# Quantized feed-forward: each engine's instructions in a written order, five turns deep, and square roots taken from the square sums

## The chip, the core and the metric

The kernel runs as one program on one core of a Trainium2 chip. A core has several engines with instruction queues of their own: TensorE (PE in the profile; PEld are its weight loads), VectorE (DVE), ScalarE (ACT), GpSimd (POOL), and SyncE (SP), which here issues DMA transfers. Each engine takes its instructions in the order of its own queue, and engines wait for each other on semaphores. The metric is the time of one execution on the device in microseconds; lower is better. Beside the times there is one profiled execution, from which every row below comes.

## The reference

The whole computes a two-layer network on `x` (64 x 64 tokens of 256 features): a conditioned scan with attention, a feed-forward, an RNN with a state-space block, and two mixtures of experts. The change is in the first feed-forward, whose input is the residual modulated by a condition and whose two linear layers work on values and weights quantized on the fly:

```python
def _L0_cond2_ref(Efou, y, weight):
    ys = y * (1.0 / np.sqrt(np.float32(weight.shape[0])))
    d = jax.lax.rsqrt(jnp.einsum('bi,io->bo', ys * ys, weight * weight) + 1e-08)
    return jnp.einsum('bsi,io->bso', Efou * ys[:, None, :], weight) * d[:, None, :]

def _L0_ffn_ref(x, norm1_w, w1, act_scale, act_bias, norm2_w, w2):
    def rmsnorm(x, w):
        v = jnp.mean(jnp.square(x), axis=-1, keepdims=True)
        return x * jax.lax.rsqrt(v + 1e-08) * w
    def activation_quant(x):
        scale = 127.0 / jnp.clip(jnp.max(jnp.abs(x), axis=-1, keepdims=True), 1e-5, None)
        return jnp.clip(jnp.round(x * scale), -128, 127) / scale
    def weight_quant(w):
        scale = 1.0 / jnp.clip(jnp.mean(jnp.abs(w)), 1e-5, None)
        return jnp.clip(jnp.round(w * scale), -1, 1) / scale
    def bitlinear(x, norm_w, w):
        return jnp.einsum('bsd,hd->bsh', activation_quant(rmsnorm(x, norm_w)), weight_quant(w))
    h = bitlinear(x, norm1_w, w1)
    h = act_scale * jnp.square(jax.nn.relu(h)) + act_bias
    return bitlinear(h, norm2_w, w2)
...
x = x + _L0_ffn_ref(_L0_cond2_ref(x, cond_1024, L0_cond2_weight), ...)
```

The hidden layer has 1024 features. There are 4096 tokens.

## The kernel before

The residual lives in SBUF as `xT`, features on the partitions, all 4096 tokens beside each other. The stage `ffn0` works on 16 *pairs*: a pair is two tiles of 128 tokens (`T = 2`, four of the 64 batch entries). For each pair seven steps run:

- `product` (lines 614 to 636): GpSimd multiplies the pair's part of `xT` by the condition into `xs` (L617); TensorE multiplies `xs` by the fp32 weight `Wc` (L628) and, beside it in the same PSUM bank, spreads the rows of `d` over the tokens with a 64-wide product against the identity (L632); ScalarE copies that `d` part to `dt` (L634), VectorE multiplies the two into `gm` (L635), and ScalarE makes the square sums of `gm` (`square_sums`, L581).
- `quantize_in`: `quantized` (L584 to L612) on `gm`, 256 wide.
- `turn`: four bf16 transposes on TensorE (L645) and a copy by ScalarE to `qT` (L647).
- `up`: for each of the two tiles two 512-wide bf16 products with `w1q` (L655), each evicted by ScalarE with a Relu scaled by `back1` (L656); then ScalarE's square (L658) and VectorE's activation scale and bias (L659); after both tiles the square sums of `h` (L581).
- `quantize`: `quantized` on `h`, 1024 wide.
- `turn_back`: for each tile eight transposes (L670) and ScalarE's copy to `q2T` (L671).
- `down`: for each tile eight products with `w2q` (L678), ScalarE's scaled eviction `o` (L680), two fp32 transposes (L682); then VectorE adds the result to `xT` (L684) and SyncE sends the pair to `x_mid` in HBM (L685).

`quantized` holds small columns of per-token numbers in one tile `st`: GpSimd makes `v`, the mean square (L592); ScalarE its root (L593); VectorE the reciprocal (L594); five GpSimd instructions refine that by one Newton step and make the largest allowed scale `most` (L595 to L599). VectorE multiplies by the norm weight (L600), takes the largest magnitude (L601), makes the scale from it and `most` (L603, L604); GpSimd makes the factor `back` of the later eviction (L605, L606); VectorE scales and rounds (two L609) and writes the bf16 result (L611).

The steps are written as a pipeline seven turns deep: in a turn, `down` of one pair comes first and `product` of the pair six later comes last. That is the order in which the program asks for the work. The framework's scheduler then sets the order in each engine's queue from its own estimate of when things are ready, so the queues interleave several pairs differently from the text. PSUM has two rings of four banks, `ps` (`product`, `turn`, `up`) and `acc` (`turn_back`, `down`). Tiles of `f2` have two buffers, those of `f3` (`st`, `h`) three.

The stage before is attention, whose memory the stage takes over; behind it comes the RNN, which needs the whole residual (its first products, L723, read all of `xT`).

Of the kernel before, what the change touches and what calls it, by code (L numbers as in the profile page):

```python
# [13 lines left out]
F32 = mybir.dt.float32  # L14
BF16 = mybir.dt.bfloat16
I32 = mybir.dt.int32
AF = mybir.ActivationFunctionType
ALU = mybir.AluOpType
AX = mybir.AxisListType
PSUM = bass.MemoryType.PSUM  # L20

P = 128
B, L, D = 64, 64, 256
# [53 lines left out]
def bank(g, shape=(P, CH), dt=F32, tag="ps"):  # L77
    tag = g.tag or tag
    return g.psum.tile(list(shape), dt, tag=tag, name=tag)
# [452 lines left out]
def ffn0_prepared(g, pool, w):  # L532

    nc = g.nc
    ones = pool.tile([P, P], F32, name="ones")
    nc.gpsimd.memset(ones, 1.0)
    w.w1q, w.m1, one = ternary(g, pool, w.w1, ones, "w1")
    w.w2q, w.m2, two = ternary(g, pool, w.w2, ones, "w2")

    w.ys = ys = pool.tile([P, KD, B], F32, name="ys")  # L540
    ysq = pool.tile([P, KD, B], F32, name="ysq")
    wsq = pool.tile([P, KD, D], F32, name="wsq")
    w.d = d = pool.tile([B, D], F32, name="d")
    d2 = pool.tile([B, 2, D], F32, name="d2")

    def squares():
        nc.vector.tensor_scalar(ys, g.condT, 1.0 / math.sqrt(D), None, ALU.mult)
        nc.vector.tensor_mul(ysq, ys, ys)
        nc.vector.tensor_mul(wsq, w.Wc, w.Wc)

    def sums():
        ps = bank(g)
        for k in range(KD):
            nc.tensor.matmul(ps[:B, :D], ysq[:, k, :], wsq[:, k, :], start=(k == 0), stop=(k == KD - 1))
        nc.vector.tensor_scalar(d2[:, 0, :], ps[:B, :D], EPS, None, ALU.add)

    return chain(one, two, (squares, sums)), (lambda: rsqrt(nc, d2[:, 0, :], d, d2[:, 1, :]),)


def ffn0(g, w):  # L560


    nc, tc = g.nc, g.tc
    F = w.F
    NF = F // P
    T = 2
    TP = T * P
    NP = NT // TP
    BP = TP // L
    with (  # L570
        tc.tile_pool(name="f1", bufs=1) as p1,
        tc.tile_pool(name="f2", bufs=2) as p2,
        tc.tile_pool(name="f3", bufs=3) as p3,
    ):
        w1q, m1, w2q, m2, ys, d = w.w1q, w.m1, w.w2q, w.m2, w.ys, w.d

        def square_sums(x, n):
            ss = p2.tile([P, T], F32, name=f"ss{n}")
            for t in range(T):
                junk = p1.tile([P, n], BF16, name=f"junk{n}")  # L580
                nc.scalar.activation(junk, x[:, t, :], AF.Square, accum_out=ss[:, t : t + 1])  # L581
            return ss

        def quantized(x, ss, wn, mean, n):  # L584

            st = p3.tile([P, 7, T], F32, name=f"st{n}")  # L590
            v, rs, t, most, am, sc, back = (st[:, i, :] for i in range(7))
            nc.gpsimd.tensor_scalar(v, ss, 1.0 / n, EPS, ALU.mult, ALU.add)  # L592
            nc.scalar.activation(rs, v, AF.Sqrt)  # L593
            nc.vector.reciprocal(rs, rs)  # L594
            nc.gpsimd.tensor_mul(t, rs, rs)  # L595
            nc.gpsimd.tensor_mul(t, t, v)
            nc.gpsimd.tensor_scalar(t, t, -0.5, 1.5, ALU.mult, ALU.add)
            nc.gpsimd.tensor_mul(rs, rs, t)
            nc.gpsimd.tensor_scalar(most, rs, 127.0 / 1e-5, None, ALU.mult)  # L599
            nc.vector.tensor_tensor(x, x, wn.unsqueeze(1).to_broadcast([P, T, n]), ALU.mult)  # L600
            nc.vector.tensor_reduce(am, x, AX.X, ALU.max, apply_absolute_value=True)  # L601

            nc.vector.reciprocal(sc, am)  # L603
            nc.vector.scalar_tensor_tensor(sc, sc, 127.0, most, ALU.mult, ALU.min)  # L604
            nc.gpsimd.tensor_mul(back, am, rs)  # L605
            nc.gpsimd.tensor_scalar(back, back, 1e-5, mean, ALU.max, ALU.mult)  # L606
            q = p2.tile([P, T, n], BF16, name=f"q{n}")
            for i in range(T):
                nc.vector.tensor_scalar(x[:, i, :], x[:, i, :], sc[:, i : i + 1], MAGIC, ALU.mult, ALU.add)  # L609

            nc.vector.tensor_scalar(q, x, MAGIC, 127.0, ALU.subtract, ALU.min)  # L611
            return q, back  # L612

        def product(p, v):
            tok = ts(p, TP)
            xs = p2.tile([P, KD, BP, L], F32, name="xs")
            nc.gpsimd.tensor_tensor(  # L617
                xs,
                g.xT[:, :, tok].rearrange("p k (b l) -> p k b l", l=L),
                ys[:, :, ts(p, BP)].unsqueeze(3).to_broadcast([P, KD, BP, L]),  # L620
                ALU.mult,
            )
            xs2 = xs.rearrange("p k b l -> p k (b l)")
            gm = p2.tile([P, T, D], F32, name="gm")
            for t in range(T):
                ps = bank(g, (P, 2, D))
                for k in range(KD):
                    nc.tensor.matmul(ps[:, 0, :], xs2[:, k, ts(t, P)], w.Wc[:, k, :], start=(k == 0), stop=(k == KD - 1))  # L628

                for j in range(2):  # L630
                    b = p * BP + 2 * t + j
                    nc.tensor.matmul(ps[ts(j, L), 1, :], g.ident[:B, b : b + 1].to_broadcast([B, L]), d, start=True, stop=True)  # L632
                dt = p2.tile([P, D], F32, name="dt")
                nc.scalar.copy(dt, ps[:, 1, :])  # L634
                nc.vector.tensor_mul(gm[:, t, :], ps[:, 0, :], dt)  # L635
            v.gm, v.ss1 = gm, square_sums(gm, D)

        def quantize_in(p, v):
            v.q1, v.back1 = quantized(v.gm, v.ss1, w.n1, m1, D)

        def turn(p, v):
            pt = bank(g, (P, KD, TP), BF16)
            for t in range(T):
                for k in range(KD):
                    nc.tensor.transpose(pt[:, k, ts(t, P)], v.q1[:, t, ts(k, P)], g.identb)  # L645
            v.qT = p2.tile([P, KD, TP], BF16, name="qT")
            nc.scalar.copy(v.qT, pt)  # L647

        def up(p, v):
            v.h = p3.tile([P, T, F], F32, name="h")  # L650
            for t in range(T):
                for f in range(F // CH):
                    ps = bank(g)
                    for k in range(KD):
                        nc.tensor.matmul(ps, v.qT[:, k, ts(t, P)], w1q[:, k, ts(f, CH)], start=(k == 0), stop=(k == KD - 1))  # L655
                    nc.scalar.activation(v.h[:, t, ts(f, CH)], ps, AF.Relu, scale=v.back1[:, t : t + 1])  # L656
                h = v.h[:, t, :]
                nc.scalar.activation(h, h, AF.Square)  # L658
                nc.vector.tensor_scalar(h, h, w.act[:, 0:1], w.act[:, 1:2], ALU.mult, ALU.add)  # L659
            v.ss = square_sums(v.h, F)  # L660

        def quantize(p, v):
            v.q2, v.back2 = quantized(v.h, v.ss, w.n2, m2, F)

        def turn_back(p, v):
            v.q2T = p2.tile([P, T, NF, P], BF16, name="q2T")
            for t in range(T):
                pt = bank(g, (P, NF, P), BF16, tag="acc")
                for f in range(NF):
                    nc.tensor.transpose(pt[:, f, :], v.q2[:, t, ts(f, P)], g.identb)  # L670
                nc.scalar.copy(v.q2T[:, t], pt)  # L671

        def down(p, v):
            po = bank(g, (P, KD, TP), tag="acc")
            for t in range(T):
                ps = bank(g, tag="acc")
                for f in range(NF):
                    nc.tensor.matmul(ps[:, :D], v.q2T[:, t, f, :], w2q[:, f, :], start=(f == 0), stop=(f == NF - 1))  # L678
                o = p2.tile([P, D], F32, name="o")
                nc.scalar.activation(o, ps[:, :D], AF.Copy, scale=v.back2[:, t : t + 1])  # L680
                for k in range(KD):
                    nc.tensor.transpose(po[:, k, ts(t, P)], o[:, ts(k, P)], g.ident)  # L682
            x = g.xT[:, :, ts(p, TP)]
            nc.vector.tensor_add(x, x, po)  # L684
            nc.sync.dma_start(g.x[:, :, ts(p, TP)], x)  # L685

        stages = (product, quantize_in, turn, up, quantize, turn_back, down)
        pairs = [SimpleNamespace() for _ in range(NP)]
        for turn_ in range(NP + len(stages) - 1):
            for i in reversed(range(len(stages))):  # L690
                p = turn_ - i
                if 0 <= p < NP:
                    stages[i](p, pairs[p])

# [1408 lines left out]
```

## Time and profile before

| what | us |
|---|---|
| median of 3 runs (lowest, highest) | 2876.07 (2875.18, 2876.6) |
| the profiled execution | 2877.2 |
| its span, first to last instruction | 2875.5 |
| busy in the span: PE, DVE, ACT, POOL | 2415.3, 1766.7, 1413.8, 1306.9 |
| ffn0: first L617 to last L684 | 381.9 to 638.4 |
| ffn0's start, 382 to 439: PE, DVE, ACT busy of 57 (granted clock) | 41.8, 37.7, 37.8 (0.73) |
| middle, 439 to 562: of 123 | 93.1, 101.1, 91.7 (0.78) |
| end, 562 to 639: of 77 | 53.5, 63.7, 57.9 (0.89) |

The stage is 9% of the span. A row of a timeline gives the start, the duration, the engine, the line, the operation, what it writes and reads, and in brackets how long the engine had been idle and what ended that. Displayed durations of instructions that follow each other on one engine overlap a little, because the next one starts while the last one's results drain; times from start to start are therefore shorter than durations, except where an instruction needs the one just before it. TensorE's clock is granted in two steps, 1.00 and 0.50, and the tables show its mean.

### The profile page before, as it was taken

The numbers are of one execution on the slowest core, as the hardware profiler recorded it, in microseconds if no ns is written. First come the engines' busy times: TensorE is split into PE (matmuls) and PEld (weight loads), VectorE is DVE, ScalarE is ACT, GpSimd is POOL, SyncE is SP. The second block draws the span as 40 slices with busy tenths as digits, with TensorE's granted clock in tenths as the row PEclk, the third lists the DMA queues.
The fourth block names the chain that finished last, engine by engine and source line by source line (L and its number), as shares of the span: only waits on it lengthen the run. The fifth ranks groups of instructions, "written<-read, shape, count | busy, mean of one in ns | idle before, by whom it ended". The sixth has DMA issues, their size and how long they took to land.

```text
span 2875.5 us, 34868 instructions
## 1 busy us (share of the span) xinstructions
PE 2415.3 (84%) x12142; PEld 1706.9 (59%) x12156; DVE 1766.7 (61%) x3059; ACT 1413.8 (49%) x2410; POOL 1306.9 (45%) x1125
## 2 busy tenths in 40 slices
PE   4989977779666878887787888868988999999996
PEld 4634334448334555555455555656876778888885
DVE  0567648870299989898987889894345443323322
ACT  0567557764556676767475767643333222222220
POOL 0023334540178676767477777772746341111110
PEclk9979987889576999999899899979999999999997
DMA  9999710010022212121122122222787846555555
GB/s 229 374 359 339 237 25 19 15 61 11 30 74 66 75 63 76 56 84 56 70 63 90 65 76 86 85 81 76 232 288 261 312 170 254 218 191 208 203 190 181
DMA packets 183077, 406.07 MB, mean 141 GB/s; under 512 B 25312, under 2 KB 89056, under 8 KB 177520
## 3 DMA queue, kind: packets, MB, share of 16 engines
q1 hardware_dynamic: 169456, 366.80, 38.1%
q0 software_dynamic: 13440, 36.98, 3.3%
q8 instruction: 98, 1.61, 0.2%
q14 instruction: 83, 0.68, 0.1%
HBM read 280.76 MB, written 144.98 MB: 148 GB/s over the span
## 4 chain that ended last, share of the span: by engine, by line
PE 43%; DVE 20%; ACT 9%; issue 8%; POOL 5%; DMA 3%; SPq 0%; DVEq 0%; POOLq 0%; ACTq 0%
DVE hb L1009 12%; PE ps L1603 11%; PE acc L1501 8%; DVE hb L1011 3%; PE mq L1739 2%; PE yp L1025 2%; PE ps L1570 2%; PE mp L906 2%; DVE xc L851 2%; PE mq L1755 1%; PE ps L628 1%; PE ps L745 1%; POOL hb L970 1%; PE acc L745 1%; PE ps L1611 1%
## 5 line engine op out<-in xcount | busy, mean ns | idle before, releaser
L970 POOL TENSOR_TENSOR hb<-dx,Bn 128x1024 f32<-128x1024 f32 x256 | 601.3, 2359 | 262.3 <-PE yp L1025 257.6
L1009 DVE TENSOR_TENSOR_SCAN hb<-dA,hb 128x512 f32<-128x512 f32 x512 | 602.6, 1208 | 32.9 <-ACT dA L977 30.4
L977 ACT ACTIVATE dA<-delta,A 128x504 f32<-128x504 f32 x512 | 344.3, 683 | 308.0 <-DVE hb L1009 304.9
L1025 PEld LDWEIGHTS yp<-ident,hb 128*128 128x128 f32 x2048 | 269.1, 152 | 185.0 <-issue 147.0
L1011 DVE TENSOR_TENSOR hb<-hb,cb 128x1024 f32<-128x1024 f32 x256 | 312.0, 1219 | 84.3 <-PE cb L922 67.2
L1603 PE MATMUL ps<-gxT,w 128*128 128x256 f32 (+1 forms) x1600 | 324.1, 361 | 0.8 <-DVE gxT L1478 0.8
L1603 PEld LDWEIGHTS ps<-gxT,w 128*128 128x128 f32 x1600 | 276.3, 190 | 46.4 <-issue 12.4
L1025 PE MATMUL yp<-ident,hb 128*128 128x128 f32 x2048 | 303.3, 292 | 0.0
L1739 PE MATMUL mq<-x,moe_s 128*128 128x256 f32 x896 | 250.3, 412 | 48.0 <-ACT up L1746 27.4
L1277 POOL DMA_INDIRECT ffn_y<-gy,to x72 | 69.2, 961 | 429.0 <-ACT gy L1503 416.5
L1739 PEld LDWEIGHTS mq<-x,moe_s 128*128 128x128 f32 x896 | 169.0, 204 | 112.5 <-ACT up L1746 35.8
L1607 DVE TENSOR_TENSOR gh<-gs,ps 128x256 f32<-128x256 f32 (+1 forms) x200 | 78.7, 393 | 206.8 <-ACT gs L1606 206.8
L922 PE MATMUL cb<-parts,pick 80*128 80x512 bf16 x256 | 105.7, 413 | 114.8 <-DVE hb L1011 99.8
L1501 PE MATMUL acc<-w,gh 128*128 128x256 f32 (+1 forms) x864 | 189.1, 389 | 0.0
L1606 ACT ACTIVATE gs<-ps 128x256 f32<-128x256 f32 (+1 forms) x200 | 72.4, 362 | 230.3 <-PE ps L1603 227.7
L1503 ACT ACTIVATE gy<-acc,wt 128x256 f32<-128x256 f32 x152 | 67.0, 472 | 236.6 <-PE acc L1501 231.6
L1501 PEld LDWEIGHTS acc<-w,gh 128*128 128x128 f32 (+1 forms) x864 | 146.2, 190 | 30.4 <-issue 13.4
L426 POOL TENSOR_TENSOR E<-E,z 128x1024 f32<-128x1024 f32 x32 | 61.6, 1925 | 201.1 <-DVE z L425 116.9
L1755 PE MATMUL mq<-moe_s,sh 128*128 128x256 f32 x448 | 116.7, 399 | 6.6 <-ACT up L1746 6.6
L444 PE MATMUL out<-oT,M 128*128 128x512 f32 x256 | 117.9, 604 | 1.5 <-ACT oT L437 1.5
L1755 PEld LDWEIGHTS mq<-moe_s,sh 128*128 128x128 f32 x448 | 83.8, 197 | 42.4 <-issue 20.6
L1277 POOL DMA_INDIRECT moe_y<-gy,to x80 | 77.3, 966 | 69.4 <-ACT gy L1503 51.7
(462 smaller groups left out, 4497.4 us busy)
## 6 DMA issues: line engine op xcount, KB each, us to landing
w<-ffn_w SPq DMA_DIRECT2D x40, 2176.0 KB, 9.1
Bn<-B SPq DMA_DIRECT2D x128, 512.0 KB, 3.6
moe_x<-fill SPq DMA_DIRECT2D x130, 260.0 KB, 5.9
ffn_x<-fill SPq DMA_DIRECT2D x129, 260.0 KB, 6.0
w<-moe_w SPq DMA_DIRECT2D x48, 512.0 KB, 4.8
ffn_w<-in_ffn_W_dram SPq DMA_DIRECT2D x16, 640.0 KB, 8.8
gx<-moe_x SPq DMA_DIRECT2D x32, 260.0 KB, 4.9
gx<-ffn_x SPq DMA_DIRECT2D x32, 260.0 KB, 9.2
```

Of the source, the lines that this page charges most:

```text
L444: nc.tensor.matmul(ps, M[:, o, ts(k, P)], v.o[:, o], start=(o == 0), stop=(o == H // 2 - 1))
L922: nc.tensor.matmul(t, pick[:, n : n + 1].to_broadcast([rows, P]), v.parts, start=True, stop=True)
L970: nc.gpsimd.tensor_mul(hb, vs[c].dx[p], Bn[:, n % NB, :].unsqueeze(1).to_broadcast([P, PI, CH]))
L977: nc.scalar.activation(decays[s][i][:, :, 1:], seq(vs[c].delta[p][:, i, :])[:, :, 1:], AF.Exp, scale=w.A[:, p * PI + i, n : n + 1],)
L1009: ins = nc.vector.tensor_tensor_scan(h, dA[i].rearrange("p b l -> p (b l)"), h, 0.0, ALU.mult, ALU.add)
L1011: ins = nc.vector.tensor_tensor(hb, hb, cb.unsqueeze(1).to_broadcast([P, PI, CH]), ALU.mult)
L1025: nc.tensor.matmul(yp[i][:, t, :], hb[:, i, ts(t, P)], g.ident, start=(n == 0 and t == 0), stop=(n == S - 1 and t == CH // P - 1), is_tran ...
L1277: i = self.g.nc.gpsimd.indirect_dma_start(out=self.y, out_offset=bass.IndirectOffsetOnAxis(ap=to, axis=0), in_=y, in_offset=None)
L1501: nc.tensor.matmul(po[s], h, w, start=(i == 0), stop=(i == n - 1))
L1603: nc.tensor.matmul(ps[:, j, :], v.w12[:, k, ts(j * (full + 1) + i, P)], v.xT[:, k, :], start=(k == 0), stop=(k == KD - 1))
L1739: nc.tensor.matmul(ps[:, i % 2, :], w[:, k, ts(i, P)], xu[:, k, :], start=(k == 0), stop=(k == KD - 1))
L1755: nc.tensor.matmul(ps[:, t, :], h[:, i, ts(t, P)], self.s2[:, i, :], start=(i == 0), stop=(i == NS - 1))
```

## The change

Every instruction of the stage is now asked for through `InOrder`, a wrapper that marks it with a token of its engine, so that the scheduler keeps the written order on that engine. The steps are split finer and written out in one fixed order (`turn_at`): `product` into `spread`, `product` and `modulated`; `turn` into `turn` and `turned`; `up` by tile; the act scaling (`scaled`) and the square sums (`sums`) on their own; `down` into `down`, `lie_down` and `add`. The pipeline is five turns deep. `quantized` loses its front part: `roots` has ScalarE take the root from the square sums, with the mean's factor as scale and a column of `EPS` as bias, while GpSimd still makes `v`; `better` does the reciprocal and the five GpSimd steps, and can be placed apart: for `h` it stands, with the next pair's `spread`, between the norm product and the search for the largest magnitude. All sizes, tiles, buffers and counts of instructions are as before, but for the column `eps` and its memset.

```diff
+    w.eps = pool.tile([P, 1], F32, name="eps")
+    nc.gpsimd.memset(w.eps, EPS)
...
+class InOrder:
+    def __init__(self, tc, engine, name):
+        self.tc, self.engine, self.name = tc, engine, f"in_order_{name}"
+
+    def __getattr__(self, op):
+        def ask(*args, **kwargs):
+            ins = getattr(self.engine, op)(*args, **kwargs)
+            self.tc.stamp_issue_order_token(ins.ins, self.name)
+            return ins
+
+        return ask
...
+        te, ve, se, pe = (InOrder(tc, getattr(nc, n), n) for n in ("tensor", "vector", "scalar", "gpsimd"))
...
-        def quantized(x, ss, wn, mean, n):
+        def roots(ss, n):
             st = p3.tile([P, 7, T], F32, name=f"st{n}")
+            v, rs, t, most = (st[:, i, :] for i in range(4))
+            se.activation(rs, ss, AF.Sqrt, bias=w.eps, scale=1.0 / n)
+            pe.tensor_scalar(v, ss, 1.0 / n, EPS, ALU.mult, ALU.add)
+            return st
+
+        def better(st):
+            v, rs, t, most = (st[:, i, :] for i in range(4))
+            ve.reciprocal(rs, rs)
+            pe.tensor_mul(t, rs, rs)
+            pe.tensor_mul(t, t, v)
+            pe.tensor_scalar(t, t, -0.5, 1.5, ALU.mult, ALU.add)
+            pe.tensor_mul(rs, rs, t)
+            pe.tensor_scalar(most, rs, 127.0 / 1e-5, None, ALU.mult)
+
+        def quantized(x, st, wn, mean, n, *between):
             v, rs, t, most, am, sc, back = (st[:, i, :] for i in range(7))
-            nc.gpsimd.tensor_scalar(v, ss, 1.0 / n, EPS, ALU.mult, ALU.add)
-            nc.scalar.activation(rs, v, AF.Sqrt)
-            nc.vector.reciprocal(rs, rs)
-            nc.gpsimd.tensor_mul(t, rs, rs)
...
+            ve.tensor_tensor(x, x, wn.unsqueeze(1).to_broadcast([P, T, n]), ALU.mult)
+            for other in between:
+                other()
+            ve.tensor_reduce(am, x, AX.X, ALU.max, apply_absolute_value=True)
...
-        stages = (product, quantize_in, turn, up, quantize, turn_back, down)
-        for turn_ in range(NP + len(stages) - 1):
-            for i in reversed(range(len(stages))):
...
+        def turn_at(n):
+            def root_big(p, v):
+                v.st2 = roots(v.ss, F)
+
+            def root_small(p, v):
+                v.st1 = roots(v.ss1, D)
+
+            def quantize(p, v):
+                rest = (lambda: better(v.st2)), (lambda: at(spread, n + 1))
+                v.q2, v.back2 = quantized(v.h, v.st2, w.n2, m2, F, *rest)
+
+            def quantize_in(p, v):
+                better(v.st1)
+                v.q1, v.back1 = quantized(v.gm, v.st1, w.n1, m1, D)
+
+            def sums(p, v):
+                v.ss = square_sums(v.h, F)
+
+            at(quantize_in, n - 1)
+            at(down, n - 4)
+            at(root_big, n - 3)
+            if 0 <= n - 3 < NP:
+                at(quantize, n - 3)
+            else:
+                at(spread, n + 1)
+            at(up, n - 2, 0)
+            at(lie_down, n - 4)
+            at(product, n)
+            at(up, n - 2, 1)
+            at(turn, n - 1)
+            at(turned, n - 1)
+            at(modulated, n)
+            at(root_small, n)
+            at(turn_back, n - 3)
+            at(add, n - 4)
+            at(scaled, n - 2)
+            at(sums, n - 2)
+
+        at(spread, 0)
+        for n in range(NP + 4):
+            turn_at(n)
```

`at(stage, p)` runs a step if pair `p` exists. `spread` is the old L617, `modulated` the old L634, L635 and the square sums, `lie_down` the old L682 for both tiles, `add` the old L684 and L685, `scaled` the old L659 for both tiles.

## The prediction

> **What bounds the kernel now.** The change touches one stage, the first feed-forward (ffn0), so I first cut the trace to it: the first `xs` (L617) starts at 381.87 us and the last residual add (L684) starts at 637.72 and takes 0.69, so the stage is 256.5 us of a 2875.5 us span. The RNN behind it needs the whole residual, so every microsecond of the stage is on the path; all instructions outside ffn0 and its seam with the RNN stand in the same order in both builds. The first add starts at 439.4 (57.5 us in); the other fifteen follow in 198.3, 13.2 us each.
>
> Then engine busy time by stretches, cut where the granted clock changes (columns: stretch, length, busy us and count on PE, PEld, DVE, ACT, POOL, then clock, DMA share, GB/s):
> ```profile
> 437.41:454.48 17.07, 12.93 (x96) 7.94 (x95) 15.30 (x28) 15.76 (x34) 10.88 (x23) 1.00 0.07 25
> 454.48:468.13 13.65, 10.45 (x38) 5.87 (x39) 10.05 (x17) 7.46 (x15) 4.87 (x15) 0.50 0.03 9
> 468.13:485.19 17.06, 12.34 (x90) 7.44 (x90) 15.56 (x27) 15.64 (x33) 10.26 (x19) 1.00 0.09 31
> 485.19:498.85 13.66, 10.83 (x39) 6.10 (x41) 10.07 (x19) 7.09 (x15) 5.29 (x17) 0.50 0.01 1
> ```
> Two pairs take 30.7 us, 15.4 each. At full clock DVE and ACT are both about 90% busy; at half clock both idle and PE sets the pace. DVE's work is only (15.30 + 10.05)/2 = 12.7 us a pair, so some 2.7 us a pair is waiting. The same view in windows of 3.41 us shows what goes before a drop of the clock:
> ```profile
> 440.82:444.24 3.42, 1.87 (x23) 1.52 (x20) 3.42 (x3) 3.42 (x7) 3.09 (x5) 1.00 0.22 77
> 451.06:454.48 3.42, 1.50 (x18) 1.09 (x18) 3.42 (x9) 2.42 (x5) 1.70 (x4) 1.00 0.13 46
> 454.48:457.89 3.41, 0.77 (x4) 0.58 (x5) 3.41 (x3) 3.38 (x7) 1.19 (x6) 0.50 0.09 31
> 461.30:464.71 3.41, 3.41 (x11) 1.73 (x9) 2.90 (x6) 1.33 (x3) 0.00 (x0) 0.50 0.00 0
> ```
> PE busy 1.87 kept the full clock, 1.50 lost it; and a window full of `product` (461.30) did not yet bring it back. The waits of 437.41 to 498.85 name what stands idle: PE for `q2T`, and VectorE for GpSimd's small chain:
> ```profile
> PE acc L678 <- ACT q2T L671: 11.0, 4, 4.0
> DVE st L604 <- POOL st L599: 10.0, 3, 3.6
> ```
>
> **The change, part by part.** *VectorE's turn.* Nothing is added to or taken from VectorE; the order becomes fixed, and one pair's dependent steps now follow each other, where before another pair's work stood between them. So I price steps start to start, from places where the trace has them in that order:
> ```profile
> 394.08 0.17 DVE L603 RECIPROCAL st<-st 128x2 f32<-128x2 f32 x1
> 394.91 0.16 DVE L604 SCALAR_TENSOR_TENSOR st<-st 128x2 f32<-128x2 f32 x1 [0.67 <-POOL st L599]
> 395.11 0.62 DVE L609 TENSOR_SCALAR gm<-gm,st 128x256 f32<-128x256 f32 x2
> 395.76 0.43 DVE L611 TENSOR_SCALAR q<-gm 128x512 bf16<-128x512 f32 x1
> 625.88 2.26 DVE L601 TENSOR_REDUCE st<-h 128x2 f32<-128x2048 f32 x1
> 628.18 0.17 DVE L603 RECIPROCAL st<-st 128x2 f32<-128x2 f32 x1
> 628.45 0.16 DVE L604 SCALAR_TENSOR_TENSOR st<-st 128x2 f32<-128x2 f32 x1
> 628.64 1.42 DVE L609 TENSOR_SCALAR h<-h,st 128x1024 f32<-128x1024 f32 x2
> 630.10 1.23 DVE L611 TENSOR_SCALAR q<-h 128x2048 bf16<-128x2048 f32 x1
> ```
> Small half (`quantize_in`): reciprocal 0.08, norm product 0.70 (0.67 and the 0.04 by which a dependent step starts after its input ends), then 1.40 to the scale: GpSimd's five steps take 1.37 (466.43 to the waiting L604 at 467.80 in the timeline) and cannot begin under the norm product; reduce and reciprocal cover 0.97 of it. Then 0.20, 0.65 and 0.34 (0.42 less overlap): 3.4. Large half: norm product 2.19 (613.82 to 616.01), reciprocal 0.08, reduce 2.30, 0.27, 0.19, 1.46, 1.14 (624.07 to 625.21): 7.6. Two `gm` products 0.74, add 0.60, two act scalings 1.45: 2.8. **Sum 13.8 us a turn**: 1.1 more than the bare work, because overlaps are lost.
>
> *GpSimd under VectorE.* A step of 0.2 us waits while VectorE multiplies two SBUF tensors:
> ```profile
> 470.52 2.27 DVE L600 TENSOR_TENSOR h<-h,n 128x2048 f32<-128x2048 f32 x1
> 470.68 2.16 POOL L595 TENSOR_TENSOR st<-st 128x2 f32<-128x2 f32 x1 [1.77 <-DVE st L594]
> ```
> The new order puts the large half's five steps (1.37) and `spread` (1.04) under the reduce (2.30), in whose time the trace has such steps at 0.19 to 0.23. With the 0.13 before them they end 2.5 us after the reciprocal, before the scalings at 2.8: no cost. Without that cover it is the 3.6 us wait shown above. The chain of the small half has no such cover; its 0.4 is in the sum.
>
> *The roots.* ScalarE takes them from `ss` with scale and bias; the GpSimd step for `v` stays, off the path. ACT's waits for L592 were 12.5 us in ten cases over the stage. In the new ACT order each root stands behind its own sums, so it neither waits nor lets others wait; the root row is 0.21 before and I take it unchanged (bounds: the shortest sqrt row 0.19, the table load of 1.28 if each root needed one; the built ACT list has two loads there, as before). VectorE's reciprocal comes 2 us later, so nothing hangs on it.
>
> *ScalarE's turn, and the new wait.* Group means by pair: four L656 of 0.69, two L658 1.06, two large sums 1.28, two small 0.62, two `q2T` 1.0, two `o` 0.49, two `dt` 0.38, `qT` 0.59, two roots 0.21: 13.4, less 0.11 overlap for each of 23 instructions, 10.9. In the fixed order ACT's second pair of Relus (`up`, t = 1) waits behind `lie_down` and `product` on PE, which wait for ACT's `o`. PE's part, by the chain of waits:
> ```profile
> 384.10 0.58 PE ps L632 x4
> 490.59 1.81 PE ps L628 x4
> 492.40 1.05 PE ps L632 x4
> 505.62 1.07 PE ps L628 x4
> ```
> `product` is two of each: 3.3 at full clock, 5.7 at half. With `lie_down` (0.66; 1.07) and `up`'s first two matmuls (0.6; 1.0) PE needs 4.5 or 7.8 after `o`; ACT has a root, two Relus and a square meanwhile, 2.2. So ACT's loop is 10.9 + 2.3 = 13.2 at full clock, under VectorE's 13.8, and 16.5 at half. Queued behind that Relu are `qT`, `dt`, `q2T`: PE's `down` and VectorE's `gm` are late next.
>
> *The clock.* Between `turn` and `down` PE has about 4.5 us with 1.06 of transposes (sixteen L670). That holds a window under 1.50 in most turns. I take one window of half clock a turn: 1.7 us of PE work lost, 0.6 covered by VectorE's longer turn, 1.1 where it falls on the loop, some half of the time: 0.55. Bounds: 0 (clock kept), and 1.3 if half clock keeps the 44% of the time that it has now (0.44 of 16.7 - 13.8; PE at half clock needs 15.7 of matmuls and waits 1.0 for `q2T`). **Turn 14.35.**
>
> The Trainium skill (TensorE: Matmul & The Clock Gate, Part 1) has the clock fall after an idle window of about 3.4 us. The window with 1.50 of work that lost it was not idle, so the row decides; by the page no turn would lose the clock, and the stage would be the full-clock sum below.
>
> *Fill and drain.* The first add comes in the fifth turn instead of the seventh. First small `q` ends 11.4 us in (392.90 + 0.41), of which 8.0 is ahead of `quantize_in`; the second turn 8 (three table loads of 1.28 in the first two), the third 7.5 (ACT: one `up`, sums of `gm`), the fourth VectorE's 3.4 + 7.6 + 2.2, the fifth 12.4 to the add: 49, say 50 with half clock (now 58.2). Then twelve turns. At the end two turns without the small half, 12.5 each (7.6 + 0.6 + 1.45, then large sums and root, 2.8), and 6 from the last `q` to the add (now 7.1).
>
> **Sum:** 50 + 12 x 14.35 + 31 = 253.2 against 256.5: 3.3 us less. Span 2872.2; the profiled run is 1.7 above its span and 1.1 above the median shown, so **2873 us**.
>
> **Rivals.** *A, the clock holds:* 49 + 12 x 13.8 + 30 = 244.6, 11.9 less: 2864. For it: PE has one block of 8 to 9 us a turn. Against: the row at 1.50. Any turn under 14.15 gives more than 0.2%. *B, slower, the loop of `o`, `product` and the second Relus at half clock:* with today's 44%, 15.1 a turn, 51 + 181 + 32 = 264, 7.5 more: 2884. It decides from 15.0 a turn, a half-clock share of 41%. For it: `product` alone does not bring the clock back (461.30). Against: `down` and `up`, bf16, now stand in the same block. *C, the order is not kept:* the built lists of each engine follow the written order, so I give it nothing.
>
> **Chances.** 0.2% is 5.75 us, about what a measurement tells from no change. Forecast (within) 0.47; A and what lies between 0.38; B 0.15. Range 2862 to 2886: A less 2 for the RAW steps that I may have counted too dear, B plus 2. The forecast's own is 2868 to 2878.
>
> **What would show it.** Adds 14.0 to 14.8 us apart with VectorE over 90% busy; first add 50 us in; L604's wait for GpSimd near 0.4 a turn; ACT idle before the second Relus some 2 us. Wrong if VectorE idles for `gm` or ACT waits for `product` 4 us and more in most turns (B), or PEclk is 1.0 (A).

## The result, and the profile after

| | before | after |
|---|---|---|
| median, us (lowest, highest; 12 runs each) | 2874.01 (2869.98, 2876.74) | 2874.57 (2862.54, 2879.91) |
| ratio | | 0.9999, 95% interval 0.9989 to 1.001 |
| the profiled execution, its span | 2877.2, 2875.5 | 2871.99, 2869.8 |
| ffn0, first `xs` to last add | 256.5 | 260.1 |
| rest of the span behind the stage | 2237.1 | 2228.0 |
| first add / adds 1 to 12, one pair | 58.2 / 14.66 | 51.8 / 14.81 |
| last four adds apart | 10.0, 14.5, 6.9, 5.6 | 13.0, 13.1, 12.9, 6.4 |
| at half clock within the stage | 102.4 | 85.3 |

The time did not change. In the traces the stage itself is 3.6 us longer. The profiled run of after is nevertheless 5.2 us shorter, since the rest of its span, whose instructions did not change, took 9.1 us less. That is scatter and not the change: in the ten traces of before, after and e1 to e9 below this rest lies anywhere from 2228.0 to 2237.1, and it is 2237.0 in e1, which has the change too. So the total of one run says little about this stage: below, the stage is read from the trace, beside the ratio of all runs. How far one trace can be trusted is seen from a control below, which has the order of before on four engines: 253.8 against 256.5. Differences under 3 us in the stage are not read as anything, and the 3.6 us are hardly more; the interval of the ratio allows from 3.2 us less to 2.9 us more.

"One pair" is (end of the 12th add − end of the first)/11. "At half clock" is the time in which TensorE was granted a clock of 0.50. In after, all instructions of the stage stand under L570, the line of the wrapper, so they are told apart by tile. First three consecutive turns in the middle, from add to add (columns: stretch, length, busy us and count on PE, PEld, DVE, ACT, POOL, clock, DMA share, GB/s):

```profile
492.10:507.70 15.60, 11.55 (x64) 7.03 (x64) 13.03 (x22) 12.08 (x24) 7.21 (x17) 0.78 0.05 17
507.70:522.20 14.50, 10.40 (x64) 6.35 (x64) 13.07 (x22) 11.92 (x25) 7.76 (x17) 0.88 0.06 20
522.20:536.40 14.20, 10.18 (x64) 6.36 (x64) 13.00 (x22) 11.80 (x24) 7.21 (x17) 0.88 0.05 18
```

VectorE works 13.0 us in every turn, whatever the clock; the turn is 14.2, 14.5 or 15.6, and the longest has the lowest clock. The waits of the stage in before (total, number, longest):

```profile
DVE st L604 <- POOL st L599: 20.2, 8, 3.6
ACT st L593 <- POOL st L592: 12.5, 10, 2.8
DVE gm L635 <- ACT dt L634: 8.3, 5, 2.7
ACT h L656 <- PE ps L655: 0.7, 3, 0.3
```

and in after:

```profile
PE acc L570 <- ACT q2T L570: 34.6, 16, 3.6
ACT h L570 <- PE ps L570: 28.4, 20, 2.6
DVE gm L570 <- ACT dt L570: 19.8, 16, 2.7
DVE st L570 <- POOL st L570: 5.0, 16, 0.3
```

VectorE's wait for GpSimd's small chain has fallen from 20.2 us in eight cases to 5.0 in sixteen, 0.3 each. Two others have taken its place: ScalarE waits for the Relus' products, and VectorE for `dt`. VectorE's own timeline of one turn shows where:

```profile
496.57 2.29 DVE L570 TENSOR_TENSOR h<-h,n 128x2048 f32<-128x2048 f32 x1
498.78 0.16 DVE L570 RECIPROCAL st<-st 128x2 f32<-128x2 f32 x1
498.90 2.29 DVE L570 TENSOR_REDUCE st<-h 128x2 f32<-128x2048 f32 x1
501.22 0.17 DVE L570 RECIPROCAL st<-st 128x2 f32<-128x2 f32 x1
501.49 0.16 DVE L570 SCALAR_TENSOR_TENSOR st<-st 128x2 f32<-128x2 f32 x1
501.69 1.44 DVE L570 TENSOR_SCALAR h<-h,st 128x1024 f32<-128x1024 f32 x2
503.16 1.23 DVE L570 TENSOR_SCALAR q<-h 128x2048 bf16<-128x2048 f32 x1
506.29 0.76 DVE L570 TENSOR_TENSOR gm<-ps,dt 128x256 f32<-128x256 f32 x2 [1.91 <-ACT dt L570]
```

The large half runs from the norm product to `q` without a bracket: no step waits for GpSimd. Then VectorE stands 1.91 us for `dt`, which ScalarE could not copy sooner, because it stood before the second pair of Relus (in the same turn: 2.59 idle, ended by PE's `ps`).

### The profile page after: what moved, and what is told of

It reads as the page before. It is cut to its first block, busy times and chain, and to the rows that moved or that the text cites. A ratio compares the mean times of both kernels' runs of the same rounds, so it can differ in the third digit from the quotient of the medians.

```text
span 2869.8 us, 34936 instructions
## 1 busy us (share of the span) xinstructions
PE 2400.5 (84%) x12156; PEld 1706.4 (59%) x12156; DVE 1776.5 (62%) x3059; ACT 1421.9 (50%) x2410; POOL 1303.4 (45%) x1126
## 4 chain that ended last, share of the span: by engine, by line
PE 43%; DVE 21%; ACT 8%; issue 7%; POOL 4%; DMA 3%; SPq 0%; DVEq 0%; POOLq 0%; ACTq 0%
DVE hb L1093 12%; PE ps L1687 11%; PE acc L1585 8%; DVE hb L1095 3%; PE ps L570 2%; PE acc L570 2%; PE ps L1654 2%; PE yp L1109 2%; PE mp L990 2%; PE mq L1823 2%; POOL hb L1054 2%; DVE xc L935 2%; PE mq L1839 1%; PE ps L829 1%; PE acc L829 1%
## 5 line engine op out<-in xcount | busy, mean ns | idle before, releaser
L1361 POOL DMA_INDIRECT moe_y<-gy,to x80 | 77.4, 967 | 69.6 <-ACT gy L1587 52.5
```

Source lines behind the costliest of these rows:

```text
L1361: i = self.g.nc.gpsimd.indirect_dma_start(out=self.y, out_offset=bass.IndirectOffsetOnAxis(ap=to, axis=0), in_=y, in_offset=None)
```

## The experiments

Each kernel ran in three rounds beside runs of before. e1 to e9 ran on two chips where before took 2872.5 us, e10 and e11 on one where it took 2911.4, e12 and e13 on one with 2907.9. On the last two the rest of the span behind the stage is 30 to 46 us longer, while VectorE's and ScalarE's long instructions of the stage have the same durations (norm product 2.26 to 2.29). Before itself was profiled with the runs of the result alone. Ratios are always to the runs of before on the same chip (for after, those of the result).

| kernel | median | ratio to before (95%) | stage | first add | one pair | half clock |
|---|---|---|---|---|---|---|
| before (e1 to e9) | 2872.5 | | 256.5 | 58.2 | 14.66 | 102.4 |
| after | 2874.57 | 0.9999 (0.9989–1.001) | 260.1 | 51.8 | 14.81 | 85.3 |
| e1_warm | 2865.03 | 0.997 (0.9952–0.9988) | 249.8 | 51.0 | 13.88 | 20.5 |
| e2_up_first | 2870.03 | 0.9998 (0.998–1.0016) | 255.3 | 59.9 | 13.61 | 105.8 |
| e3_free_order | 2859.88 | 0.9961 (0.9946–0.9975) | 242.6 | 43.6 | 13.70 | 78.5 |
| e4_root_only | 2852.59 | 0.9944 (0.9922–0.9966) | 234.3 | 55.6 | 12.46 | 64.9 |
| e5_old_root | 2886.81 | 1.0042 (1.0027–1.0057) | 269.7 | 52.5 | 15.44 | 95.6 |
| e7_no_cover | 2888.5 | 1.0048 (1.0035–1.006) | 276.2 | 54.9 | 15.59 | 122.9 |
| e8_root_warm | 2839.29 | 0.9882 (0.9846–0.9919) | 227.2 | 54.8 | 12.29 | 20.5 |
| e9_before_warm | 2874.61 | 0.9998 (0.9982–1.0014) | 259.2 | 55.9 | 15.05 | 75.1 |
| e10_vector_free | 2933.24 | 1.0077 (1.0045–1.0108) | 271.6 | 45.7 | 15.42 | 112.6 |
| e11_vector_only | 2926.56 | 1.0056 (1.0034–1.0079) | 268.4 | 54.7 | 15.25 | 116.1 |
| e12_same_order_old_root | 2912.56 | 1.0012 (0.9994–1.0031) | 253.8 | 57.0 | 14.53 | 85.3 |
| e13_same_order_new_root | 2896.67 | 0.9943 (0.9922–0.9965) | 247.1 | 55.6 | 13.65 | 88.7 |

### The clock: e1

After, with TensorE work that computes nothing in front of the first transposes of `turn_back` and of the first product of `down`:

```diff
                 pt = bank(g, (P, NF, P), BF16, tag="acc")
+                if t == 0:
+                    for f in range(3 * NF):
+                        te.transpose(pt[:, f % NF, :], g.identb, g.identb)
...
                 ps = bank(g, tag="acc")
+                if t == 0:
+                    for f in range(NF):
+                        te.matmul(ps[:, :D], g.identb, w2q[:, f, :], start=True, stop=True)
```

> The changed kernel with TensorE work added where it has little: 24 transposes of the identity before each pair's first turn_back, into the bank that the real ones then overwrite, and eight more products in down's first bank, overwritten too. 1.3 and 0.9 us a turn at full clock, where TensorE waits anyway. Theory 1, half clock is what lifts the turn from VectorE's 13.8 to the 14.8 measured: no half clock after the fill, adds 13.7 apart, stage 246 instead of 260, the whole 13 less than the changed kernel. Theory 2, the clock only shows that TensorE waits and the turn is held by the written order itself (VectorE's waits for GpSimd and for gm): the clock is full, but adds stay 14.5 or more apart and the stage 257 or more.

Half clock fell from 85.3 to 20.5 us and the pair from 14.81 to 13.88. The windows of the clock in after show what lost it (columns as above, windows of 3.41 us):

```profile
489.02:492.43 3.41, 1.07 (x16) 0.90 (x16) 2.87 (x5) 3.13 (x10) 0.18 (x1) 1.00 0.00 0
492.43:495.85 3.42, 2.40 (x12) 1.72 (x13) 3.00 (x9) 3.39 (x6) 2.15 (x8) 0.50 0.23 77
495.85:499.26 3.41, 3.41 (x14) 2.08 (x13) 3.38 (x6) 2.86 (x7) 2.63 (x3) 0.50 0.00 0
499.26:502.67 3.41, 3.41 (x19) 1.83 (x18) 3.23 (x5) 1.27 (x2) 2.26 (x7) 1.00 0.00 0
502.67:506.09 3.42, 2.34 (x24) 1.40 (x22) 1.68 (x2) 2.90 (x5) 0.00 (x0) 1.00 0.00 0
506.09:509.50 3.41, 0.42 (x4) 0.39 (x5) 3.21 (x7) 3.13 (x9) 0.78 (x2) 1.00 0.22 77
509.50:512.91 3.41, 3.41 (x16) 2.13 (x15) 2.96 (x8) 3.38 (x8) 2.33 (x8) 0.50 0.01 2
```

Here a window with 1.07 or 0.42 us of work is followed by half clock; one with 2.34 keeps it. A half window with 3.41 brings the clock back, one with 2.40 does not, and so the drop at 492.43 lasts two windows. (In before, the full half window at 461.30 that the forecast shows did not bring it back, so busy time alone does not decide this.) In e1 the same place in the turn is filled:

```profile
499.48:502.89 3.41, 2.87 (x48) 2.67 (x47) 3.19 (x6) 3.13 (x8) 0.22 (x1) 1.00 0.00 0
502.89:506.31 3.42, 2.44 (x23) 1.83 (x21) 3.19 (x7) 3.39 (x7) 1.78 (x6) 1.00 0.23 77
```

Holding the clock gained 0.93 us a turn and 10.3 us in the stage. VectorE still works 211.5 us, as in after.

### The loop of ScalarE and TensorE: e2

After, with `product` behind the second `up`, the `turn` and the copy to `qT`:

```diff
-            at(product, n)
             at(up, n - 2, 1)
             at(turn, n - 1)
             at(turned, n - 1)
+            at(product, n)
```

> The changed kernel with product moved behind up's second tile, turn and turned, on TensorE and with it dt and gm as before behind them. Theory 1, the loop is o, lie_down, product, the second Relus: ScalarE's idle 2.0 before the second Relus goes, product lies beside the Relus and squares, half clock hurts less, adds 13.8 apart, stage 252. Theory 2, the loop runs elsewhere (product to dt to gm to VectorE's next turn): VectorE waits longer for gm, adds 14.8 or more apart, stage 260 or more.

ScalarE's wait for the Relus' products fell from 28.4 to 1.6 us, and the pair to 13.61, although half clock rose to 105.8 us:

```profile
ACT h L570 <- PE ps L570: 1.6, 8, 0.2
```

The windows of the clock show here that a drop can follow a fuller window, too:

```profile
464.54:467.95 3.41, 2.02 (x15) 1.12 (x14) 3.24 (x7) 2.27 (x5) 1.11 (x3) 1.00 0.00 0
467.95:471.36 3.41, 2.46 (x20) 1.91 (x18) 3.38 (x8) 3.29 (x8) 1.29 (x3) 0.50 0.23 77
```

So the clock cost time in after only because it stretched this loop; with the loop broken, VectorE's fixed row sets the turn. But the first add comes 8.1 us later, since `product` of each pair is late in its turn (the third pair's `gm` is ready 9.2 us later than in after), and only 4.8 of the 13 us gained on the way are left in the stage.

### Order against roots: e3, e4 and e5

e3 is after without the tokens: the same text, but the scheduler sets the order.

```diff
             ins = getattr(self.engine, op)(*args, **kwargs)
-            self.tc.stamp_issue_order_token(ins.ins, self.name)
             return ins
```

> The changed kernel without the order tokens: the same text, five turns deep, roots from the square sums, but the scheduler sets the order on each engine. Theory 1, the written order costs VectorE 1.1 a turn in lost overlaps and the rest in the loop with TensorE: interleaving returns, adds 13.2 to 13.6 apart, stage 240 to 249. Theory 2, the order is what keeps the turn together: adds 15 apart as before at half clock, stage 256 to 264.

e4 is before with nothing but the new root, in the free order:

```diff
+    w.eps = pool.tile([P, 1], F32, name="eps")
+    nc.gpsimd.memset(w.eps, EPS)
...
+            nc.scalar.activation(rs, ss, AF.Sqrt, bias=w.eps, scale=1.0 / n)
             nc.gpsimd.tensor_scalar(v, ss, 1.0 / n, EPS, ALU.mult, ALU.add)
-            nc.scalar.activation(rs, v, AF.Sqrt)
```

> The kernel before with one part of the change: ScalarE takes each root straight from its square sums, GpSimd's mean square goes behind it. Nothing else. By the prediction, which gave the roots no gain on the path: stage 253 to 257, the whole within 3 us. The rival: in the scheduler's order ScalarE's wait for GpSimd's step, up to 2.3 long when VectorE holds GpSimd off, was on the path, and it goes: adds 12.9 apart, stage 238 to 245, the whole 12 to 16 less than before.

e5 is after with the old root:

```diff
-            se.activation(rs, ss, AF.Sqrt, bias=w.eps, scale=1.0 / n)
             pe.tensor_scalar(v, ss, 1.0 / n, EPS, ALU.mult, ALU.add)
+            se.activation(rs, v, AF.Sqrt)
```

> The kernel after with its written order kept, but with the root as before: GpSimd first makes v from the square sums, and ScalarE's Sqrt waits for it. With e4_root_only (before with the new root alone: stage 234.3 us against 256.5) this completes the table of order against roots. Theory 1, the forecast's (the roots cost nothing in the written order, since the GpSimd step of 0.2 us has time behind ScalarE's other work): stage 258 to 263 us, 14.7 to 15.0 us a pair, whole kernel 2870 to 2878. Theory 2 (a ScalarE that waits for GpSimd is dear in any order, because the GpSimd step is itself stretched to 2.2 us or held behind VectorE's work): stage 272 to 286 us, 15.7 to 16.5 us a pair, a wait of ScalarE for GpSimd's st of 0.8 us or more a turn, whole kernel 2884 to 2898.

The stage in the four combinations of the two parts of the change:

| | old root | new root |
|---|---|---|
| scheduler's order | 256.5 (before) | 234.3 (e4) |
| written order | 269.7 (e5) | 260.1 (after) |

The new root gains 22.2 us in the free order and 9.6 in the written one. The written order costs 13.2 with the old root and 25.8 with the new. The change is both, −22.2 + 25.8 = +3.6: no small effect, but two large ones that cancel. e3 says the same from the other side: without the tokens the text of after takes 17.5 us less. It also splits the 25.8: 17.5 are the held order, and the other 8.3 (242.6 against 234.3) come with the text itself, five turns deep instead of seven and with finer steps. e4 came out below both of its expected ranges, e5 between its two.

Why the old root is dear in the written order stands in e5's timeline:

```profile
502.71 2.29 DVE L570 TENSOR_TENSOR h<-h,n 128x2048 f32<-128x2048 f32 x1 [0.47 <-ACT junk L570]
502.76 2.29 POOL L570 TENSOR_SCALAR st<-ss 128x2 f32<-128x2 f32 x1 [1.15 <-ACT junk L570]
...
505.09 0.20 ACT L570 ACTIVATE st<-st 128x2 f32<-128x2 f32 x1 [1.39 <-POOL st L570]
...
505.33 0.17 DVE L570 RECIPROCAL st<-st 128x2 f32<-128x2 f32 x1 [0.32 <-ACT st L570]
```

The GpSimd step that makes `v` has two columns to work on and takes 0.19 us where nothing is in its way. Here it starts 0.05 us behind VectorE's norm product, takes 2.29 and ends 0.05 behind it. ScalarE's root waits 1.39 for it, and the Relus behind the root start late. In all, ScalarE waited 32.4 us for GpSimd in the stage:

```profile
ACT st L570 <- POOL st L570: 32.4, 30, 1.7
```

The Trainium skill (SBUF — State Buffer, "SBUF: two separate sides") says that a VectorE instruction with two SBUF inputs and a GpSimd instruction that reads SBUF exclude each other for the whole length of one of them; the two rows above are that, at 2.29 us. In after `v` is stretched in the same way in nearly every turn (2.29 in fifteen of sixteen large halves), but only GpSimd's own next steps stand behind it, and those wait for the reciprocal anyway, which VectorE reaches after the norm product.

### The cover under the reduction: e7

After, with GpSimd's chain of the large half and `spread` put behind the reduction:

```diff
             ve.tensor_tensor(x, x, wn.unsqueeze(1).to_broadcast([P, T, n]), ALU.mult)
+            ve.tensor_reduce(am, x, AX.X, ALU.max, apply_absolute_value=True)
             for other in between:
                 other()
-            ve.tensor_reduce(am, x, AX.X, ALU.max, apply_absolute_value=True)
```

> The kernel after with GpSimd's chain of the large half and the xs product put behind VectorE's reduction instead of under it. The forecast priced these steps at nothing because the reduction (2.2 us and more) hides them, and named 3.6 us as the cost if that cover is gone. Theory 1 (the cover is what hides them): VectorE's second reciprocal and the scalar_tensor_tensor wait for GpSimd about 1 us or more a turn, 15.3 to 16.0 us a pair, stage 268 to 278 us, whole kernel 2880 to 2892. Theory 2 (ScalarE's loop sets the pace and VectorE has 1 us of waits a turn to give): 14.7 to 15.1 us a pair, stage 258 to 264, whole kernel within 3 us of after.

```profile
506.23 2.29 DVE L570 TENSOR_REDUCE st<-h 128x2 f32<-128x2048 f32 x1
508.43 0.28 DVE L570 RECIPROCAL st<-st 128x2 f32<-128x2 f32 x2
508.67 0.47 POOL L570 TENSOR_TENSOR st<-st 128x2 f32<-128x2 f32 x2 [2.43 <-DVE st L570]
...
510.04 0.98 DVE L570 SCALAR_TENSOR_TENSOR st<-st 128x2 f32<-128x2 f32 x1 [1.33 <-POOL st L570]
```

VectorE waits 1.33 us there, and its instruction is itself longer (0.98 instead of 0.16) beside GpSimd's `xs` product. The stage is 16.1 us longer than in after. The cover is what hides the chain, and it is worth 1.0 us a pair (16.1/16) as the stage stands: of the 2.1 us that VectorE loses at this place (1.33 and 0.82), shorter waits for `dt` give back 0.8 a pair (19.8 us in after, 6.8 in e7). Half clock rose too, from 85.3 to 122.9 us; what that adds is not parted from the rest.

### Is the root's gain the clock? e8 and e9

Since e4 also spent 37.5 us less at half clock than before, the added TensorE work of e1 was put into both: e8 is e4 with it, e9 is before with it.

> Before with the new root alone (e4_root_only) and with the same added TensorE work as in e1_warm. Theory 1 (the half clock still costs there as it did in the written order: 10.3 us for 64.8 us less at half clock): half clock in the stage from 64.9 us to 20 to 40, stage 226 to 231 us, 11.8 to 12.2 us a pair, whole kernel 2844 to 2850. Theory 2 (VectorE's 12.1 us of work a pair is the bound by now): stage 232 to 237, whole kernel within 4 us of e4_root_only's 2852.6. Theory 3 (the added matmuls, placed freely, stand in the way of the real ones): stage above 238.

> Before with the added TensorE work alone and nothing else changed. It asks how much of e4_root_only's 22.2 us can be the clock, since that kernel also had 37.5 us less at half clock. Theory 1 (the waits for GpSimd bound before, the clock comes second): half clock in the stage from 102.4 us to 30 to 50, stage 247 to 256 us, waits of ScalarE for GpSimd (12.5 us) and of VectorE for GpSimd (20.2 us) about as before. Theory 2 (the clock is most of it: a lower clock made the chain late, and the root change only happened to raise it): stage 236 to 244 us, and the waits for GpSimd shrink by half.

Windows over the whole stage of e9, and then of e8:

```profile
383.20:642.40 259.20, 215.57 (x1560) 142.95 (x1560) 198.91 (x340) 187.28 (x373) 132.64 (x299) 0.86 0.08 23
```

```profile
377.90:605.10 227.20, 192.92 (x1560) 130.05 (x1560) 200.84 (x340) 188.42 (x373) 152.32 (x300) 0.95 0.09 26
```

e9 has the mean clock of e4 (0.86) and takes 259.2 us, no less than before: a clock like e4's does not by itself bring e4's time. It missed the ranges of both theories, and it is no clean test: its half clock fell by 27 us only, PE was busy for 28 us more than in before (215.6 for 187.7), and VectorE still waits 15.9 us for GpSimd's chain. In e8, where VectorE's wait for this chain is small (3.1 us), the held clock gives 7.1 us for 44.4 us less at half clock. At that rate the 37.5 us of e4 would be worth 6 of its 22.2 us, an estimate; most of the gain is not the clock. VectorE is then busy for 200.8 of 227.2 us, 88%. e8 is the fastest version found: 2839.29 us, 1.2% below before (0.8 to 1.5%).

### The root in an unmoved order: e12 and e13

In e4 the scheduler also moved other instructions. To part the two, the order that before has on PE, VectorE, ScalarE and GpSimd in this stage was written down instruction by instruction and held with tokens: e12 with the old root, as a control, e13 with the new one.

```diff
+ORDER = (
+    "IJIJKKLJMbJIKKLJMbdJtKKLJMfJvIKxKhLjMblbnfprzBFDFdtHNhjNvlNxnNOpJrJzBKFDKFLJHJMIKKLPMPQPbPQPbdPtRPvQ"
...
+        for c in ORDER:
+            line, s = int(kinds[c][:3]), kinds[c][3:]
...
+            if s:
+                quantizing(line, s, p, pairs[p], i)
+            else:
+                step(line, p, pairs[p], i)
```

> Before with its own order of instructions on TensorE, VectorE, ScalarE and GpSimd in this stage, written out by hand one by one; the old root. It is the control for the next run. If the order alone decides, and not the buffers that the hand-written list takes in another sequence, the stage is 254 to 259 us, as the 256.5 of before, with waits of ScalarE for GpSimd's st of 11 to 14 us; a stage beyond that would say that the list doesn't stand for before.

> The same hand-written order of before, with the root taken by ScalarE from its own square sums: no instruction changes its place. e4_root_only made this change where the order is free, and the stage fell from 256.5 to 234.3 us, but the order there moved too. Theory 1 (the wait for GpSimd's step itself, and what stands behind it, is the gain): stage 234 to 241 us. Theory 2 (the shorter path lets the work be interleaved otherwise, and that is most of it): stage 244 to 255 us, near the 9.6 us that the roots were worth in the written order of after, or less.

The list of e12 is the order that the trace of before shows on these four engines, and e13 keeps it on each of them. The control stands for before: 253.8 us, just under its range, and ScalarE's waits for GpSimd 12.7 (12.5 in before). Waits in e13:

```profile
PE acc L570 <- ACT q2T L570: 24.6, 15, 3.2
...
DVE st L570 <- POOL st L570: 11.6, 7, 2.8
```

and the same two in e4:

```profile
PE acc L680 <- ACT q2T L673: 10.0, 10, 2.1
...
DVE st L606 <- POOL st L601: 5.8, 5, 1.8
```

With no instruction moved the root gains 6.7 us against the control in the trace (9.4 against before). Half clock did not fall with it (88.7 for the control's 85.3), so this gain is not the clock's. ScalarE no longer waits for GpSimd, and VectorE's wait for GpSimd's chain falls from 19.4 to 11.6, since with an earlier root the chain can start sooner. In e4 it falls to 5.8, and PE's wait for `q2T` to 10.0. By the traces, then, the root without any move is worth 30 to 42% of e4's gain, as the second theory had it, and the moved order the rest. The whole times do not bear that out: e13's median is 15.9 us below e12's, measured beside it, and its ratio (0.35 to 0.78% below before, 10 to 23 us) is that of e4. The profiled run of e13 was the slowest of its five. So the root pays without a move; whether the moved order adds anything is open.

### Which engine's order costs? e10 and e11

e10 holds the order on all engines but VectorE, e11 on VectorE alone:

```diff
         te, ve, se, pe = (InOrder(tc, getattr(nc, n), n) for n in ("tensor", "vector", "scalar", "gpsimd"))
+        ve = nc.vector
...
+        te, se, pe = nc.tensor, nc.scalar, nc.gpsimd
```

> The kernel after with the order held on TensorE, ScalarE and GpSimd, and free on VectorE alone. The written order cost 25.8 us against the same roots in before's free order (260.1 against 234.3 in the stage), and the same stage functions without any order gave 242.6. Theory 1 (it is VectorE's fixed row of instructions, in which nothing can step past a waiting one, that costs): stage 242 to 249 us, VectorE's waits for dt and for GpSimd below 0.6 us a pair together, whole kernel 2858 to 2866. Theory 2 (it is the loop of ScalarE and TensorE with the product behind the turned-back output; VectorE only follows): stage 255 to 262 us, 14.4 to 14.9 us a pair, ScalarE's wait before the second Relus 2 us a turn as in after.

> The mirror of it: the order held on VectorE alone, free on TensorE, ScalarE and GpSimd. Theory 1 (VectorE's fixed row costs): stage 253 to 262 us, 13.5 to 14.9 us a pair, VectorE 13 us of work a pair and nearly no idle time. Theory 2 (the loop of ScalarE and TensorE costs): stage 241 to 249 us, ScalarE's wait before the Relus below 1 us a pair, whole kernel 2857 to 2865.

Neither theory holds. Both are slower than the full written order (271.6 and 268.4 against 260.1 in the stage) and than the free one (242.6), and the ratios to before say the same (1.0077 and 1.0056 against 0.9999 and 0.9961). Each has waits of its own: in e10 ScalarE still stands 25.3 us for the Relus' products and VectorE 11.4 for GpSimd, in e11 the first is down to 1.8, but VectorE stands 23.6 us for ScalarE's roots, in all 16 pairs. So the cost of the written order could not be put on one engine in this way, and which one it is stays open. What the traces do show is that VectorE's own work grows: 211.5 us busy in after against 200.5 in e4, with the same 340 instructions.

## Why the prediction was right, and where it was not

**The time.** 2873 was forecast, 2874.57 measured, within the case given the most. That it came so near is in part luck: the forecast was 3 us less than before, and nothing was gained. Its sum for the stage was 253.2, and the trace has 260.1. The 6.9 us are: fill 51.8 for 50 (+1.8); twelve turns 175.9 for 172.2 (+3.7: eleven of 14.81, and a twelfth of 13.0 which already lacks work); drain 32.4 for 31 (+1.4). The rest of the span happened to be 9.1 shorter in that run, and before's median was 2 us lower over all twelve runs than over the three known to the forecast.

**VectorE's turn, 13.8.** Right. With the clock held (e1) the pair takes 13.88, with the loop broken (e2) 13.61. VectorE works 13.0 to 13.1 a turn, and the wait for GpSimd in the small half is 0.31, where 0.4 was priced. The 1.1 a turn of lost overlaps is there: 11 us more VectorE time in the stage than in e4, 0.7 a pair, and the waits between dependent steps.

**GpSimd under VectorE.** Right that it costs nothing as placed. Without the cover it cost 1.0 us a pair (e7). The forecast named the 3.6 us wait as that price, and that was the wrong row: in before's timeline, ahead of that wait, GpSimd's queue was held 5.34 us by an `xs` product that waited for PE, and the chain stood behind it. The wait without cover is 1.33.

```profile
465.43 1.04 POOL L617 TENSOR_TENSOR xs<-xT,ys 128x512 f32<-128x512 f32 x1 [5.34 <-PE ps L628]
466.43 0.19 POOL L595 TENSOR_TENSOR st<-st 128x2 f32<-128x2 f32 x1
...
467.80 0.16 DVE L604 SCALAR_TENSOR_TENSOR st<-st 128x2 f32<-128x2 f32 x1 [3.59 <-POOL st L599]
```

**The loop and ScalarE's wait.** Right: some 2 us idle before the second Relus were forecast, and the three turns have 2.59, 2.14 and 2.02. Queued behind it, `dt` makes VectorE's `gm` late, as the forecast listed as next (1.1 a turn in the middle). ScalarE's own work was priced too low: 10.9 a turn, where it is busy 35.80 of the 44.3 us, 11.9 a turn. With the clock held (e1) its wait is 1.73 where 2.3 was priced, so the loop takes 13.6 at full clock, still under VectorE's turn, but more closely than the forecast's 13.2 against 13.8 says.

**The clock, 0.55 a turn.** The mechanism was right, the size too small: e1 puts it at 0.93 (14.81 − 13.88), inside the bounds of 0 to 1.3. The step that failed is "one window of half clock a turn". Three turns of 44.3 us are thirteen windows of 3.41, and in one of the three turns the half clock lasts two windows, since the window with 2.40 us of work did not bring it back. So it is four windows in three turns, and one turn in three is 15.6. The Trainium skill's rule (TensorE: Matmul & The Clock Gate, Part 1) of an idle window before a drop would have given the full clock; the window with 1.07 us of work that lost it decides against that, as the one with 1.50 did.

**The roots, "I take it unchanged".** As a cost in the new order this was right: ScalarE has no wait for a root in after. As an account of the change it was the largest miss. The forecast read 12.5 us of waits for L592, then put no gain beside them, because the reciprocal comes later anyway. e5 gives 9.6 us for them in the written order, e13 6.7 in the old by its trace (more by the whole times), e4 22.2 where the order may follow. The forecast built its sum from the new order directly, so this gain and the order's cost of 25.8 were both inside it, unseen, and cancelled.

**Rivals.** A needed the clock to hold: it did not, and e1, which makes it hold, has A's turn (13.88 for 13.8) with 5 us more around it. B's turn of 15.1 came near, 14.81, by the mechanism that it named: half clock on the loop. By its own point (15.0 a turn) it did not decide. C did not come: VectorE's instructions stand in the written order, the same in eleven turns one after the other.

**What would show it.** First add 51.8 (50 forecast); adds 14.2 to 15.7 apart (14.0 to 14.8): the longest turn of three lies outside. VectorE is busy 39.10 of 44.3 us in the three turns, 88%, not over 90.

## What to carry to other kernels

When a change has two parts, price each alone against the kernel before, in its own order, and not only the sum in the new order: here −22 and +26 us looked like nothing, and the one part alone is a version 0.6% faster. A fixed order is a promise that no other work fills a gap, so it must be worth more than the overlap it gives up (here 17.5 us of the stage, by e3). And a small GpSimd step on the way to another engine should not stand beside a long two-input VectorE instruction; if an engine can take its input one step earlier, it spares that wait.

## What the runs showed of the hardware

- A GpSimd instruction on a 128x2 tile took 0.19 us alone. When it started 0.05 us behind VectorE's 128x2048 norm product it took 2.29, as long as the product itself, in fifteen turns of after; under VectorE's reduction of the same size the small steps stayed at 0.19 to 0.23.
- In every trace the changes of TensorE's clock lie on one grid of 3.41 us, from the first to the last, to within 0.01 us. In the middle of after the clock fell after windows of this grid with 0.42 and 1.07 us of work and stayed after 2.07 and more; at half clock it came back after windows with 2.98 and more, not after 2.40. These are no thresholds: in e2 it fell after a window with 2.02 and in e3 it stayed after one with 1.63, and in before a half window with 3.41 did not bring it back. A loop whose turn is no multiple of 3.41 us beats with this grid: 14.2, 14.5, 15.6 in after.
- 24 small transposes and 8 products in a turn that compute nothing (half clock 85.3 to 20.5 us) made the stage 10.3 us shorter where the loop over TensorE was on the path, 7.1 in e8, and nothing in e9, where ScalarE and VectorE still waited for GpSimd and TensorE worked 28 us more.
